# An attention's weights and first products moved ahead of a mixture of experts, and its pair count into another room

## The chip, the cores and the metric

One core of one Trainium2 chip. A time is the device time of one execution in microseconds (us). Engines: PE is TensorE, DVE is VectorE, ACT is ScalarE, POOL is GpSimd, SP is SyncE, which only starts transfers here. Each engine works through its own list of instructions in order, and waits for others by semaphores.

## What is computed

The input `x` is 2 x 1024 x 256. Its rows are normalized (`xn`), and three terms are added.

```python
xn = layernorm(x)
out = x + attention(xn) + ffn(xn)
# attention: tokens of 16 channels; the first 8 attend in windows of 1 x 8 tokens,
# the others in windows of 8 x 1; softmax of q.k / sqrt(8) over the 8 keys of a window,
# plus a depthwise 3x3 convolution of v; then a projection, a norm over the 16 channels, and tok + norm
# ffn: 16 experts of 176 units, of which a row uses 6
scores = sigmoid(xn @ gate.T)
choice = scores + bias                        # the two best of 4 groups, then the 6 best experts of those
w = 2.5 * scores[chosen] / sum(scores[chosen])
y = sum_e w[e] * (silu(xn @ gate_proj[e].T) * (xn @ up_proj[e].T)) @ down_proj[e].T
y += (silu(xn @ shared_gate.T) * (xn @ shared_up.T)) @ shared_down.T
```

## The kernel before

Everything runs in float32 on PE. The program is one straight list in which a scheduler may move an instruction past others on its engine, followed by a short loop at the end for what a list can't hold.

**Load stage.** The 2048 rows lie in 16 tiles of 128. `statistics` and `normalized` (L223, L234) make `xn` and its transpose `xnT`, `logits` (L251) the gate's logits. The attention's small weights come by POOL's transfers (L187 to L203). The shared expert is a generator, `shared_steps` (L263): products `pg` and `pu` on PE, a silu by ACT, `room` (L282) by DVE, and `py` (L288), which ACT writes to a tile `ysh` (L289); four transfers on POOL's queue add it to the output in HBM (L291). `meanwhile(until)` lets it run on beside other work.

**Routing** (L340 to L540) chooses the experts of each row, mostly on DVE in the tile `tmp`, and sorts the rows so that a tile of 128 rows shares six experts as far as possible. Rows with their weights go to HBM (`xw_d`).

**Experts.** `sorted_tile(t)` (L815) gathers one sorted tile by an indirect transfer on POOL's queue (L817, three buffers `xg`), PE turns it (`px_`, L821), ACT copies it, and DVE sorts its weights (L824 to L835). A *slot* is one expert on one tile: `up` (L849) makes `pr_u` on PE (L853, three PSUM buffers), ACT a silu `sg` (L855), DVE the weighted product `hms` (L856). Two slots are a unit; then `hidden` turns `hms` (`ph`, L867), ACT copies it, and the down product `pr_y` follows (L879) one unit later. There are 48 units of sorted tiles, and seven of extra pairs (a row and an expert outside of its tile's six) between tiles 7 and 13. `extras_listed` (L546) counts those pairs in parts of `tmp`; `lists_begun` (L900) then lists them in parts of a tile `ysum`, in steps of its own: ACT copies a column `spot` (L953) out of `at_`, POOL makes two comparison rows (L955, L956), PE adds up `rows_of` (L946). `ysh` and `ysum` have one tag, so they take turns in the same memory; so do `tmp` and the attention's `qk` (tag `qk`).

**Attention.** `weights_prepared` (L576) makes its weights: `qprep` from a product `pqp`, `wq`, `wp`, `rd`, then `mm` and `pb` from two products `pm`, `pbc` from a turned `pb8` (`ppb`), and `lp`. `attention(b, h)` (L653) does one quarter: ACT gathers `rows`, PE makes eight `pq` (L671), each copied by ACT in four pieces (L673 to L676), and DVE does the rest in rows of 2048 elements: `pr` (L684) and `s` (L688) four times, the highest and the exponential (L694 to L696), `pv` (L705) and `o` (L710) four times with the totals between, and `xo` (L718). PE turns `xo` (`po`, L725), ACT copies it to `oT` (L727). After the four quarters `attended` (L761) multiplies by `lp` and `wp` (`pp`, L777), and normalizes.

**The order of the two.** The experts are the main loop; a walk through the attention's steps is laid between the slots. Each step and each slot has a written cost on DVE and on PE; a step is put in when what DVE has been given is no more than `pace` times what PE has been given:

```python
    walk = all_steps()                       # L1084: the weights' eight steps first, then the quarters
    sorted_tile(0)
    meanwhile(100)                           # the rest of the shared expert
    sorted_tile(1)
...
            while step and done[0] <= pace * done[1]:
                step[2]()
                counted(step)
```

`pace` is made from the sums of these costs, so that DVE's and PE's shares end together, up to END = 72 us of PE's, which are left for the last.

## Time and profile before

| what | us |
|---|---|
| three runs | 448.25, 449.36, 454.71 |
| median | 449.36 |
| the profiled execution: its own time | 447.97 |
| its span, first to last instruction | 446.3 |
| PE busy | 393.4 |
| DVE busy | 291.5 |
| ACT busy | 214.1 |
| POOL busy | 197.9 |

A line of the profile gives a start, a length (both us), the engine, the source line, the operation, what it writes and reads with sizes, how often in a row, and in brackets how long the engine had been idle before it and what ended that wait. Busy rows by slices show each fortieth of the span, a digit for tenths. Lengths of rows that follow each other overlap by some 0.07 us, so costs below are taken from start to start where rows are dense. TensorE's granted clock was 0.987 in the mean.

### The profile page before, as it was taken

How to read it: one execution, taken by the hardware profiler on the slowest of the kernel's cores; microseconds unless marked ns; L12 is line 12 of the kernel's file. 1: busy time of each engine (PE TensorE's matmuls, PEld its weight loads, DVE VectorE, ACT ScalarE, POOL GpSimd, SP SyncE). 2: the span in 40 equal slices, each digit the busy share in tenths (PEclk: the TensorE clock that was granted, in tenths of full speed). 3: DMA queues.
4: the chain of work that ended last, by engine and by line, in shares of the span. 5: the costliest groups of instructions: out<-in, count | busy, mean ns of one | idle time of the engine just before them, and what ended most of it. 6: DMA issues, size and time to landing. Idle time of an engine off the chain costs nothing.

```text
span 446.3 us, 6293 instructions
## 1 busy us (share of the span) xinstructions
PE 393.4 (88%) x1668; PEld 246.3 (55%) x1669; DVE 291.5 (65%) x515; ACT 214.1 (48%) x535; POOL 197.9 (44%) x207
## 2 busy tenths in 40 slices
PE   0999999997899788998897999999998899979990
PEld 0435465664466555565564666656665555446670
DVE  4624958635699979289995999959999223322210
ACT  2945258322544442643635456364533657774320
POOL 7300000314273299457524245615554274779432
PEclk9999999999999999999999999999999999998997
DMA  8999941324023101101212124210332101822922
GB/s 232 338 304 321 275 154 30 64 67 86 25 71 73 32 25 34 29 23 33 38 39 60 35 43 81 47 36 24 69 90 56 22 14 57 103 68 74 126 44 24
DMA packets 40178, 37.56 MB, mean 84 GB/s; under 512 B 5300, under 2 KB 37616, under 8 KB 40112
## 3 DMA queue, kind: packets, MB, share of 16 engines
q0 software_dynamic: 11616, 13.52, 18.4%
q1 hardware_dynamic: 27472, 22.59, 16.4%
q10 hardware_dynamic: 1056, 1.05, 0.7%
q8 instruction: 15, 0.25, 0.2%
q14 instruction: 19, 0.16, 0.1%
HBM read 27.70 MB, written 12.45 MB: 90 GB/s over the span
## 4 chain that ended last, share of the span: by engine, by line
DVE 38%; PE 30%; DMA 10%; issue 8%; ACT 7%; POOL 5%; DVEq 0%; POOLq 0%; ACTq 0%; SPq 0%
DVE s L688 6%; PE pr_u L853 6%; DVE pv L705 6%; DVE pr L684 5%; DVE o L710 5%; DVE hms L856 5%; PE pp L777 4%; PE pq L671 3%; PE pr_y L879 3%; DMA out_dram<-ysum,lists 3%; PE pg L273 3%; PE py L288 2%; DMA xg<-xw_d,lists 2%; PE pu L273 2%; DMA xx<-in_x_dram 2%
## 5 line engine op out<-in xcount | busy, mean ns | idle before, releaser
L853 PE MATMUL pr_u<-w1s,xsT 128*128 x384 | 128.4, 468 | 3.4 <-DVE hms L856 2.4
L853 PEld LDWEIGHTS pr_u<-w1s,xsT 128*128 128x128 f32 x384 | 69.9, 191 | 39.4 <-issue 7.7
L994 POOL DMA_INDIRECT out_dram<-ysum,lists x30 | 57.2, 1908 | 77.4 <-ACT ysum L1040 20.3
L855 ACT ACTIVATE sg<-pr_u 128x176 f32<-128x176 f32 x110 | 34.7, 317 | 77.1 <-PE pr_u L853 70.2
L856 DVE SCALAR_TENSOR_TENSOR hms<-sg,w,pr_u 128x176 f32<-128x176 f32 x96 | 36.8, 387 | 35.5 <-ACT sg L855 35.5
L684 DVE TENSOR_TENSOR pr<-qk 128x2048 f32<-128x2048 f32 x16 | 36.6, 2288 | 17.6 <-ACT qk L673 17.2
L705 DVE TENSOR_TENSOR pv<-s,v 128x2048 f32<-128x2048 f32 x16 | 36.5, 2284 | 2.5 <-ACT s L696 2.4
L867 PE MATMUL ph<-ident,hms 128*128 128x128 f32 x165 | 31.7, 282 | 5.5 <-DVE hms L856 2.9
L688 DVE TENSOR_REDUCE s<-pr 128x256 f32<-128x2048 f32 x16 | 36.5, 2279 | 0.1
L955 POOL TENSOR_SCALAR ysum<-row_h,spot 128x128 f16<-128x128 f16 x26 | 28.0, 1094 | 19.2 <-PE rows_of L946 14.9
L710 DVE TENSOR_REDUCE o<-pv 128x256 f32<-128x2048 f32 x16 | 36.3, 2269 | 0.0
L980 POOL DMA_INDIRECT xg<-xw_d,lists x14 | 21.6, 1540 | 29.3 <-DVE hms L856 15.5
L867 PEld LDWEIGHTS ph<-ident,hms 128*128 128x128 f32 x165 | 21.5, 144 | 23.2 <-DVE hms L856 6.9
L291 POOL DMA_DIRECT2D out_dram<-ysh x4 | 3.7, 928 | 64.5 <-ACT ysh L289 64.5
L817 POOL DMA_INDIRECT xg<-xw_d,lists x16 | 19.8, 1239 | 25.4 <-PE ph L867 9.3
L879 PE MATMUL pr_y<-w2a,hT 128*128 x96 | 29.1, 386 | 0.0
L879 PE MATMUL pr_y<-wts,hT 128*128 128x256 f32 x96 | 29.0, 384 | 0.0
L879 PE MATMUL pr_y<-w2b,hT 112*128 x96 | 28.8, 381 | 0.0
L671 PE MATMUL pq<-wq,rows 128*128 128x384 f32 x64 | 25.1, 506 | 3.3 <-ACT oT L727 1.9
L869 ACT COPY hT<-ph 128x384 f32<-128x384 f32 x55 | 26.4, 480 | 2.8 <-PE ph L867 1.8
L853 PE MATMUL pr_u<-w1s,xd 128*128 x56 | 20.4, 487 | 6.6 <-ACT xd L989 6.6
L288 PE MATMUL py<-room 128*128 128x256 f32 x96 | 23.9, 387 | 0.7 <-DVE room L282 0.7
(403 smaller groups left out, 712.2 us busy)
## 6 DMA issues: line engine op xcount, KB each, us to landing
w1s<-in_w_dram SPq DMA_DIRECT2D x22, 256.0 KB, 4.4
wts<-in_w_dram SPq DMA_DIRECT2D x55, 64.0 KB, 2.1
wts<-in_w_dram SPq DMA_DIRECT2D x55, 48.0 KB, 1.7
xw_d<-xx SPq DMA_DIRECT2D x4, 544.0 KB, 4.6
w2a<-in_w_dram SPq DMA_DIRECT2D x4, 512.0 KB, 9.4
out_dram<-ysh POOLq DMA_DIRECT2D x4, 512.0 KB, 5.6
xr<-xw_d POOLq DMA_DIRECT2D x4, 512.0 KB, 5.0
out_dram<-att POOLq DMA_DIRECT2D x8, 256.0 KB, 6.4
```

What stands on the lines that cost most here:

```text
L288: nc.tensor.matmul(py, lhsT=hms[k, m][:, P * c : P * c + P], rhs=w2h[:, m], start=(m == 0), stop=(m == 2))
L671: nc.tensor.matmul(pq.rearrange("p s t c -> p (s t c)"), lhsT=rows[:, i], rhs=wq.rearrange("p s t c -> p (s t c)"), start=True, stop=True)
L684: nc.vector.tensor_tensor(pr, q_.unsqueeze(3).to_broadcast(full), k_.unsqueeze(2).to_broadcast(full), ALU.mult)
L688: nc.vector.tensor_reduce(out=s[:, n : n + NW], in_=held.pop(n), axis=AX.X, op=ALU.add)
L705: nc.vector.tensor_tensor(pr, s[:, n : n + NW].unsqueeze(3).to_broadcast(full), v[:, br, m : m + NW].unsqueeze(2).to_broadcast(full), ALU. ...
L710: nc.vector.tensor_reduce(out=o[:, n : n + NW], in_=held.pop(n), axis=AX.X, op=ALU.add)
L853: nc.tensor.matmul(pu, lhsT=lhs[:, h, :], rhs=w1s[:, :, h, bass.ds(e * I, I)], start=(h == 0), stop=(h == 1))
L855: nc.scalar.activation(sg, pu[:, 0, :], AF.Silu)
L856: nc.vector.scalar_tensor_tensor(hm[:, 0:I], sg, w, pu[:, 1, :], op0=ALU.mult, op1=ALU.mult)
L867: nc.tensor.transpose(ph[:, s, :], units[:, P * s : P * s + P], ident)
L879: nc.tensor.matmul(py, lhsT=l_, rhs=r_, start=start and n == 0, stop=stop and n == 2)
L994: nc.gpsimd.indirect_dma_start(out=out_rows, out_offset=bass.IndirectOffsetOnAxis(ap=index, axis=0), in_=ys, in_offset=None, bounds_check= ...
```

## The change

1. `weights_prepared` is unchanged in itself, but is called whole, right after the load stage and ahead of the first routing row; it was the first eight steps of the walk, beside the first experts.
2. `sorted_tile(1)` and the walk's first steps are put ahead of the rest of the shared expert (`meanwhile(100)`). `done` begins at -LEAD = -12, so the first steps come at once: `gather`, all eight `project`, then `pr`, `s`, `pr`, `s`, `pr`. LEAD is taken out of `pace`, which falls from (273.0 - 18) / (287.8 - 72) = 1.18 to (265.0 - 12 - 18) / (287.0 - 72) = 1.09.
3. `extras_listed` works in parts 4, 5, 6 and 10 of `ysum`, no longer in `tmp` and in a `work` tile; `kept` moves from part 15 to part 7.
4. `ysum` is one tile from the start, used by the shared expert too, where two tiles took turns. So later users wait for the transfers out of their own part only.
5. `at_` is laid out with its three values side by side.

In the list as built, the first six slots come after all eight `pq` of the first quarter (before, `pq` came at slots 5 and 6). Counted by `hms` rows, a quarter's DVE rows reach from 0 to 19, 21 to 40, 44 to 62 and 66 to 84, where they reached from 5 to 26, 29 to 48, 49 to 68 and 69 to 87. `po` is turned at slots 21, 44, 66 and 88, where it was 29, 49, 69 and 88. From slot 88 on the order is the same. On POOL's queue the count's iota and the first write to `at_` now stand behind the third gather, and the shared expert's fourth transfer behind the fifth gather, as before.

```diff
-        ysh = big.tile([P, 16, W], F32, name="ysh", tag="ysum")
+    ysum = big.tile([P, 16, W], F32, name="ysum")
...
+    for _ in weights_prepared():
+        pass
     table_of(AF.Sigmoid, xnT[:, 0, 15, P - 1 : P])
     logits(3)
...
-        upto, mine, more = (tmp[:, n] for n in (2, 5, 7))
+        upto, mine, more = (ysum[:, n].rearrange("p (e t) -> p e t", e=E) for n in (4, 5, 6))
...
-        pair_i = work.tile([P, E * NTL], I32, tag="xd", name="pair_i", bufs=2)
+        pair_i = ysum[:, 10].bitcast(I32)
...
-    kept = ysum[:, 15, 0 : P].bitcast(BF16).rearrange("p (e t) -> p e t", e=E)
+    kept = ysum[:, 7, 0 : P].bitcast(BF16).rearrange("p (e t) -> p e t", e=E)
...
-    at_ = room_[:, 0 : 3 * 257].rearrange("p (a n) -> p a n", a=3)
+    at_ = room_[:, 0 : 3 * 257].rearrange("p (n a) -> p a n", a=3)
...
-    def all_steps():
-        for _ in weights_prepared():
-            yield 1.0, 0.1, lambda: None
-        yield from attention_steps()
...
-    in_walk = [8 * 1.0 + 4 * (16 * 2.3 + 3.3 + 2.5 + 1.5 + 1.4) + 0.6 + 8 * 1.4, 8 * 0.1 + 4 * 6.2 + 8 * 3.9]
-    done = [0.0, 0.0]
+    in_walk = [4 * (16 * 2.3 + 3.3 + 2.5 + 1.5 + 1.4) + 0.6 + 8 * 1.4, 4 * 6.2 + 8 * 3.9]
+    LEAD = 12
+    done = [float(-LEAD), 0.0]
...
-    pace = (whole[0] - END * of_slot["six"][0] / of_slot["six"][1]) / (whole[1] - END)
+    pace = (whole[0] - LEAD - END * of_slot["six"][0] / of_slot["six"][1]) / (whole[1] - END)
...
+    def walked():
+        step = held_.pop()
+        while step and done[0] <= pace * done[1]:
+            step[2]()
+            counted(step)
+            last, step = step, next(walk, None)
+            if last[1] > 1:
+                break
+        held_.append(step)
+
+    walk = attention_steps()
+    held_ = [next(walk)]
     sorted_tile(0)
+    sorted_tile(1)
+    walked()
     meanwhile(100)
-    sorted_tile(1)
```

More of the change, by code (lines that the diff above doesn't have):

```diff
@@ L288, in down @@
                 nc.tensor.matmul(py, lhsT=hms[k, m][:, P * c : P * c + P], rhs=w2h[:, m], start=(m == 0), stop=(m == 2))
-            nc.scalar.activation(ysh[:, 4 * k + c, :], py, AF.Identity, bias=lb)
+            nc.scalar.activation(ysum[:, 4 * k + c, :], py, AF.Identity, bias=lb)
             if c == 3:
-                nc.gpsimd.dma_start(out=by_hl(out_rows)[:, 4 * k : 4 * k + 4, :], in_=ysh[:, 4 * k : 4 * k + 4, :],
+                nc.gpsimd.dma_start(out=by_hl(out_rows)[:, 4 * k : 4 * k + 4, :], in_=ysum[:, 4 * k : 4 * k + 4, :],
                                     accum_op=ALU.add)
@@ L319, in meanwhile, with weights_prepared, centred, banded @@
             spent[1] = next(share)
+    wq = const.tile([P, 3, 8, C], F32, name="wq")
+    wp = const.tile([P, 8, C], F32, name="wp")
+    lp = const.tile([P, 3, 8, C], F32, name="lp")
+    pbc = const.tile([P, 1], F32, name="pbc")
+    def weights_prepared():
+        qp8 = work.tile([4 * C, 8, C], F32, tag="xd", name="qp8", bufs=2)
+        nc.vector.tensor_copy(qp8, qpT.unsqueeze(1).to_broadcast([4 * C, 8, C]))
+        yield
+        pqp = ps_m.tile([P, 4 * C], F32, tag="m", name="pqp")
+        nc.tensor.transpose(pqp, qp8.rearrange("k t c -> k (t c)"), ident[0 : 4 * C, 0 : 4 * C])
+        qprep = const.tile([P, 4 * C], F32, name="qprep")
+        nc.vector.tensor_copy(qprep, pqp)
+        yield
+        qrep, prep = qprep[:, 0 : 3 * C], qprep[:, 3 * C : 4 * C]
+        for s in range(3):
+            nc.vector.tensor_tensor(wq[:, s], qrep[:, C * s : C * s + C].unsqueeze(1).to_broadcast([P, 8, C]),
+                                    band[:, 0, :].unsqueeze(2).to_broadcast([P, 8, C]), ALU.mult)
+        yield
+        def centred(v):
+            m = small.tile([P, 1], F32, tag="cm", name="cm")
+            nc.vector.tensor_reduce(out=m, in_=v, axis=AX.X, op=ALU.add)
+            nc.vector.tensor_scalar(m, m, 1.0 / C, None, op0=ALU.mult)
+            nc.vector.tensor_scalar(v, v, m, None, op0=ALU.subtract)
+        centred(prep)
+        centred(pb)
+        yield
+        nc.vector.tensor_tensor(wp, prep.unsqueeze(1).to_broadcast([P, 8, C]),
+                                band[:, 0, :].unsqueeze(2).to_broadcast([P, 8, C]), ALU.mult)
+        rd = const.tile([C, 5, C], F32, name="rd")
+        nc.vector.tensor_tensor(rd, prep[0:C, :].unsqueeze(1).to_broadcast([C, 5, C]),
+                                tp.unsqueeze(2).to_broadcast([C, 5, C]), ALU.mult)
+        wvr = work.tile([C, 2, 8, C], F32, tag="xd", name="wvr", bufs=2)
+        nc.vector.tensor_copy(wvr[:, 0], wvT.unsqueeze(1).to_broadcast([C, 8, C]))
+        nc.vector.tensor_copy(wvr[:, 1].rearrange("p t c -> p (t c)"), cbc.to_broadcast([C, P]))
+        yield
+        pm = ps_m.tile([P, 6, C], F32, tag="m", name="pm")
+        nc.tensor.matmul(pm[:, 0:5, :].rearrange("p d c -> p (d c)"), lhsT=wvr[:, 0].rearrange("p t c -> p (t c)"),
+                         rhs=rd.rearrange("p d c -> p (d c)"), start=True, stop=True)
+        nc.tensor.matmul(pm[:, 5, :], lhsT=wvr[:, 1].rearrange("p t c -> p (t c)"), rhs=prep[0:C, :], start=True,
+                         stop=True)
+        nc.vector.tensor_tensor(pb, pb, pm[:, 5, :], ALU.add)
+        mm = const.tile([P, 5, C], F32, name="mm")
+        nc.vector.tensor_copy(mm, pm[:, 0:5, :])
+        yield
+        ppb = ps_m.tile([P, P], F32, tag="m", name="ppb")
+        pb8 = work.tile([P, 8, C], F32, tag="xd", name="pb8", bufs=2)
+        nc.vector.tensor_copy(pb8, pb.unsqueeze(1).to_broadcast([P, 8, C]))
+        nc.tensor.transpose(ppb, pb8.rearrange("p t c -> p (t c)"), ident)
+        nc.vector.tensor_copy(pbc, ppb[:, 0:1])
+        yield
+        part = work.tile([P, 2, 8, C], F32, tag="xd", name="part", bufs=2)
+        def banded(to, tap, d):
+            nc.vector.tensor_tensor(to, mm[:, tap, :].unsqueeze(1).to_broadcast([P, 8, C]),
+                                    band[:, d, :].unsqueeze(2).to_broadcast([P, 8, C]), ALU.mult)
+        banded(lp[:, 0], 1, 0)
+        banded(part[:, 0], 0, 1)
+        banded(part[:, 1], 2, 2)
+        banded(lp[:, 1], 3, 0)
+        banded(lp[:, 2], 4, 0)
+        nc.vector.tensor_tensor(lp[:, 0], lp[:, 0], part[:, 0], ALU.add)
+        nc.vector.tensor_tensor(lp[:, 0], lp[:, 0], part[:, 1], ALU.add)
+        yield
@@ L573, in extras_listed @@
         yield
-    def weights_prepared():
-        qp8 = work.tile([4 * C, 8, C], F32, tag="xd", name="qp8", bufs=2)
-        nc.vector.tensor_copy(qp8, qpT.unsqueeze(1).to_broadcast([4 * C, 8, C]))
-        yield
-        pqp = ps_m.tile([P, 4 * C], F32, tag="m", name="pqp")
-        nc.tensor.transpose(pqp, qp8.rearrange("k t c -> k (t c)"), ident[0 : 4 * C, 0 : 4 * C])
-        qprep = const.tile([P, 4 * C], F32, name="qprep")
-        nc.vector.tensor_copy(qprep, pqp)
-        yield
-        qrep, prep = qprep[:, 0 : 3 * C], qprep[:, 3 * C : 4 * C]
-        for s in range(3):
-            nc.vector.tensor_tensor(wq[:, s], qrep[:, C * s : C * s + C].unsqueeze(1).to_broadcast([P, 8, C]),
-                                    band[:, 0, :].unsqueeze(2).to_broadcast([P, 8, C]), ALU.mult)
-        yield
-        def centred(v):
-            m = small.tile([P, 1], F32, tag="cm", name="cm")
-            nc.vector.tensor_reduce(out=m, in_=v, axis=AX.X, op=ALU.add)
-            nc.vector.tensor_scalar(m, m, 1.0 / C, None, op0=ALU.mult)
-            nc.vector.tensor_scalar(v, v, m, None, op0=ALU.subtract)
-        centred(prep)
-        centred(pb)
-        yield
-        nc.vector.tensor_tensor(wp, prep.unsqueeze(1).to_broadcast([P, 8, C]),
-                                band[:, 0, :].unsqueeze(2).to_broadcast([P, 8, C]), ALU.mult)
-        rd = const.tile([C, 5, C], F32, name="rd")
-        nc.vector.tensor_tensor(rd, prep[0:C, :].unsqueeze(1).to_broadcast([C, 5, C]),
-                                tp.unsqueeze(2).to_broadcast([C, 5, C]), ALU.mult)
-        wvr = work.tile([C, 2, 8, C], F32, tag="xd", name="wvr", bufs=2)
-        nc.vector.tensor_copy(wvr[:, 0], wvT.unsqueeze(1).to_broadcast([C, 8, C]))
-        nc.vector.tensor_copy(wvr[:, 1].rearrange("p t c -> p (t c)"), cbc.to_broadcast([C, P]))
-        yield
-        pm = ps_m.tile([P, 6, C], F32, tag="m", name="pm")
-        nc.tensor.matmul(pm[:, 0:5, :].rearrange("p d c -> p (d c)"), lhsT=wvr[:, 0].rearrange("p t c -> p (t c)"),
-                         rhs=rd.rearrange("p d c -> p (d c)"), start=True, stop=True)
-        nc.tensor.matmul(pm[:, 5, :], lhsT=wvr[:, 1].rearrange("p t c -> p (t c)"), rhs=prep[0:C, :], start=True,
-                         stop=True)
-        nc.vector.tensor_tensor(pb, pb, pm[:, 5, :], ALU.add)
-        mm = const.tile([P, 5, C], F32, name="mm")
-        nc.vector.tensor_copy(mm, pm[:, 0:5, :])
-        yield
-        ppb = ps_m.tile([P, P], F32, tag="m", name="ppb")
-        pb8 = work.tile([P, 8, C], F32, tag="xd", name="pb8", bufs=2)
-        nc.vector.tensor_copy(pb8, pb.unsqueeze(1).to_broadcast([P, 8, C]))
-        nc.tensor.transpose(ppb, pb8.rearrange("p t c -> p (t c)"), ident)
-        nc.vector.tensor_copy(pbc, ppb[:, 0:1])
-        yield
-        part = work.tile([P, 2, 8, C], F32, tag="xd", name="part", bufs=2)
-        def banded(to, tap, d):
-            nc.vector.tensor_tensor(to, mm[:, tap, :].unsqueeze(1).to_broadcast([P, 8, C]),
-                                    band[:, d, :].unsqueeze(2).to_broadcast([P, 8, C]), ALU.mult)
-        banded(lp[:, 0], 1, 0)
-        banded(part[:, 0], 0, 1)
-        banded(part[:, 1], 2, 2)
-        banded(lp[:, 1], 3, 0)
-        banded(lp[:, 2], 4, 0)
-        nc.vector.tensor_tensor(lp[:, 0], lp[:, 0], part[:, 0], ALU.add)
-        nc.vector.tensor_tensor(lp[:, 0], lp[:, 0], part[:, 1], ALU.add)
-        yield
@@ L645, in csw_block_moe @@
-    wq = const.tile([P, 3, 8, C], F32, name="wq")
-    wp = const.tile([P, 8, C], F32, name="wp")
-    lp = const.tile([P, 3, 8, C], F32, name="lp")
-    pbc = const.tile([P, 1], F32, name="pbc")
     oT = big.tile([P, 4, 2, 4, P], F32, name="oT", tag="oT")
@@ L803, in csw_block_moe @@
     xsT = big.tile([P, NTL, 2, P], F32, name="xsT", tag="xx")
-    ysum = big.tile([P, 16, W], F32, name="ysum", tag="ysum")
     xflat = ysum.rearrange("p n d -> p (n d)")[0:1, 8 * W : 8 * W + 3 * NXM].bitcast(I32)
     xrow = xflat.rearrange("p (a n) -> p a n", a=3)
-    kept = ysum[:, 15, 0 : P].bitcast(BF16).rearrange("p (e t) -> p e t", e=E)
+    kept = ysum[:, 7, 0 : P].bitcast(BF16).rearrange("p (e t) -> p e t", e=E)
     wsrt = route.tile([P, NTL, E], F32, name="wsrt")
@@ L1082, in counted @@
             done[n] += cost[n]
-    walk = all_steps()
+    def walked():
[9 more added lines that the diff above has]
+    held_ = [next(walk)]
     sorted_tile(0)
+    sorted_tile(1)
+    walked()
     meanwhile(100)
-    sorted_tile(1)
     tiles_sorted = 2
-    step = next(walk)
     laid_out = list(units())
@@ L1119, in csw_block_moe @@
             counted(of_slot[laid_out[min(u, len(laid_out) - 1)][0]])
-            while step and done[0] <= pace * done[1]:
-                step[2]()
-                counted(step)
-                last, step = step, next(walk, None)
-                if last[1] > 1:
-                    break
+            walked()
             if done_:
```

## Prediction

> **What bounds the kernel now.** I read the busy row by slices first, then VectorE's (DVE's) busy time stage by stage, then DVE in order of time.

> ```profile
> span 446.3 us, 6293 instructions
> PE   0999999997899788998897999999998899979990
> DVE  4624958635699979289995999959999223322210
> ```

> PE looks full nearly everywhere and DVE only from slice 10 on (one slice is 11.2 us). But PE's rows are pipelined and a digit hides short waits, so the middle has to be asked for by stage. I cut it at the attention's four quarters: from the first product row `pr` (L684) of a quarter to the end of its last row `xo` (L718), and the gap to the next `pr`. The columns are stretch, its length, DVE busy (instructions), granted PE clock, DMA share, GB/s.

> ```profile
> 98.00:119.05 21.05, 10.62 (x50) 0.92 0.27 59
> 119.05:179.07 60.02, 56.25 (x88) 1.00 0.19 45
> 179.07:188.05 8.98, 1.11 (x5) 1.00 0.18 28
> 188.05:238.54 50.49, 48.13 (x47) 1.00 0.17 36
> 238.54:244.27 5.73, 0.31 (x1) 1.00 0.25 59
> 244.27:292.09 47.82, 46.83 (x41) 1.00 0.27 52
> 292.09:297.96 5.87, 0.40 (x2) 1.00 0.23 34
> 297.96:345.63 47.67, 46.65 (x41) 1.00 0.26 56
> ```

> Inside a quarter DVE is 94 to 98% busy: it sets the pace. Between quarters it is idle for 5.7 to 9.0 us, while PE turns `xo` (L725), ACT copies, and PE makes the next `pq` (L671). Before the first quarter, from 98 to 119, it is half idle. So up to the last `po` at 345.68 the time is 98 + 21 + four quarters + three gaps; the last 100.6 us (after 345.68) belong to PE, ACT, POOL and the final adds, with DVE at 2 tenths.

> Why does DVE start only at 119? DVE and PE in order of time:

> ```profile
> 102.15 0.23 DVE L588 COPY qprep<-pqp 128x64 f32<-128x64 f32 x1 [5.85 <-PE pqp L586]
> 107.62 0.42 DVE L551 SCALAR_TENSOR_TENSOR ysum<-tmp,extras 128x256 bf16<-128x256 f32 x1 [2.52 <-DMA xg<-xw_d,lists]
> 110.23 0.45 PE L627 MATMUL ppb<-ident,pb 128*128 128x128 f32 x1 [2.76 <-DVE pb L626]
> 119.05 2.29 DVE L684 TENSOR_TENSOR pr<-qk 128x2048 f32<-128x2048 f32 x1 [1.72 <-ACT qk L673]
> ```

> The weights' chain waits behind the experts' start (5.85), L551 waits at 107.6, just as the last shared sum's out DMA (issued 101.95, 5.54 to land) frees the tile that `kept` lies in, PE waits for `pb8` (2.76), and `tmp`, whose room `qk` needs, is read until 116.

> **The change, part by part.**

> *Weights into the load stage.* They issue no DMA; their inputs are on the chip by 21.8 (DVE's wait at L612 ends there). DVE: from `qprep` to `rd` 102.15 to 104.95 with 0.5 of other work inside, so 2.3; then `pb`, `mm`, `pb8` 0.4 and `lp` 1.5: 4.2 us into DVE's idle 7.74 between 31.6 and 39.3. PE: `pqp` 0.27, `pm` twice 0.3, `ppb` 0.45, about 1.2 us, into a PE that is full there (5.00 busy of 33 to 38). In the new order the `room` row L284 stands behind the `lp` rows and ahead of L424, the first routing row, and waits for a `pu` that PE now ends 1.2 later (40.4 for 39.2). Routing thus starts 1.0 to 1.2 later, and its DVE chain from 40 to 57 is dense: **+1.2** as far as the first gathered tile. Without the idle cover it would be 4.2 more. From 101 to 110 the same PE work goes, with the 2.76 wait.

> *Pairs counted in ysum.* `tmp` is free once routing ends, so `qk` is. The scan now waits only for the second out DMA, long landed; the iota waits for the third (issued 83.98 before, 5.6 to land): about 91, with two gathers behind it on POOL, which wait for buffers until 92.5 anyway. Cost 0, up to 1. The strided writes of `at_` by ACT (0.41 each) and DVE have no row: between 0 and one doubling of three rows, 1.2; I take 0, the nearest rows being of equal size.

> *First products ahead of the experts.* PE: the first tile's transposes at 90.91+1.2 = 92.1, two tiles 0.8, half `pg` 0.86, two `pq` 1.3, half `pg` 0.9, two `pq` 1.3: 97.2; ACT's copies of the fourth `pq` (four at 0.16) end at 97.9. First `pr` at **98.0, 21.05 earlier**. Price: the last shared `room` row on DVE now stands behind `pr` and `s` (4.5 us), to 103.1; PE reaches `py` at 101.4 and stalls about 0.8; 20 records at 0.22 end it at 107.5. The first expert starts 6.9 later than 100.56. Queued behind: the fourth out DMA on POOL, and behind that the gather of tile 5 (about 111, landing 114; PE wants it at about 114.4). But 5.3 us of `pq`, 1.2 of weights and the waits of 2.76 and 1.27 are gone from what follows, so slot 6 (each `pr_u` of a routed expert is a slot) starts at about 120, against 124.63.

> *First quarter.* DVE's 60.0 before, plus the `room` row 0.6, plus sorting rows of four more tiles (two groups of three rows at 0.3, four copies at 0.1: 2.2), less two `hms` rows of 0.31: **62.2, +2.2**, with its 3.3 of waits kept.

> *Pace.* It falls from 1.18 to 1.09 DVE us per PE us. The order of instructions shows where this goes: a quarter's rows stand as close to the `hms` rows as before (18 or 19 slots), and the room lies in the gaps. `xo` to `po` is 3, 1, 1 and 1 slots before, and 2, 4, 4 and 4 after. In a gap PE bounds: after the last `hms` it must do `ph` 0.64, `pr_y` 1.3, two `pr_u` 2.6, `ph` and `pr_y` 1.9 ahead of `po`, 6.4, of which 1.2 lie under `xo`: 5.2 more than a gap of before with one slot. Gaps: first, with two slots for three, 7.5 for 8.98 (**-1.5**); second 10.9 for 5.73 (**+5.2**); third, with part of an extra pair (4.9 for 4.2) in it, 11.3 for 5.87 (**+5.4**); `xo` to the last `po` 5.2 for 0 (**+5.2**). The bounds are 0 (PE has run ahead) and 6.4 each. The slots done there at PE's own pace are why this is only half a loss: it is already in the sum, since the number of slots ahead of the last `po` is 88 in both.

> [...] The gathers are issued by POOL:

> ```profile
> 128.63 0.95 POOL L817 DMA_INDIRECT xg<-xw_d,lists  x1 [0.30 <-PE ph L867]
> 130.53 3.08 POOL L817 DMA_INDIRECT xg<-xw_d,lists  x1 [0.95 <-DVE wsrt L824]
> 135.61 0.95 POOL L817 DMA_INDIRECT xg<-xw_d,lists  x1 [0.74 <-PE px__1336 L821]
> ```

> 0.95 alone, 3.08 beside a `pr` row (130.51 to 132.80), 0.95 beside an `s` row (134.60 to 136.87). [...] After the change eleven gathers lie beside `pr` and `pv` rows. [...] By the trace it is hidden: three buffers mean that PE wants a tile 3.6 slots, some 9 us, after it frees the buffer, and 3.1 of issue plus 3.0 of landing are 6.1. I take 0; with the cover gone it is the slower rival.

> *Sum:* -21.05 + 2.2 - 1.5 + 5.2 + 5.4 + 5.2 = -4.5 (the +1.2 is in the 98.0). The tail has the same order in both. The profiled execution took 447.97 (1.7 around its span), so 443.4; the median shown is 449.36, 1.4 above it. I keep to the profiled execution, which two of the three runs shown lie within 1.4 of: **443.5**.

> **The rivals.**

> *The gaps close up.* If PE runs further ahead of DVE, the gaps stay at 5.8 and the last `po` follows `xo` at once: 15.8 less, 428; half of it is likelier, 436. For it: PE's plain pair of slots takes 4.2 (217.33 to 221.55) where DVE's takes 5.0 (201.20 to 206.21). Against: three `pr_u` buffers hold PE within three slots of DVE.

> *The late first expert is not made up.* If slots keep their mean pace, 245.1 from the first `pr_u` to the last `po` less 8 for the moved `pq` with its waits, the last `po` comes at 107.5 + 237 = 344.6: 447. For it: PE shows 45.3 of 47.8 busy in the third quarter. Against: the 5.0 per pair is DVE's.

> *Slower: the gathers.* If issue and landing pass the time from freeing a buffer to its use (about 9 us), each of the eleven gathers holds PE, and DVE with it: at 1.6 of the 2.1 each, 443 + 18 = 461. [...]

> **How the numbers follow.** The likeliest 0.50 (its own range 437 to 450), closing gaps 0.18, not made up 0.20, slower 0.12. From 434 to 453 leaves out the far half of the first rival (0.08) and most of the slower one (0.11). Two per cent, about what a measurement tells here, is 440.4 and 458.3. Below lie most of the first rival (0.16) and some of the likeliest (0.14), 0.30; above, the gathers, 0.11; between 0.59.

> **What would show it.** Right: the first `pr` near 98, the first `pr_u` near 107.5, no L551 or `ppb` wait, the last `po` near 341, DVE gaps of 7 to 11 us between quarters, a tail of 100 us. Wrong: `px` waits on gathers between 110 and 140, quarters much over 48 us, or routing more than 2 us late at the first gather.

## The result, and the profile after

| | us |
|---|---|
| before, median of 20 runs | 449.31 (447.73 to 454.71) |
| after, median of 20 runs | 454.41 (453.43 to 456.27) |
| after over before | 1.011, 95% interval 1.0091 to 1.0128 |
| predicted | 443.5 (434 to 453) |
| span profiled, before and after | 446.3 and 453.0 |
| first `pr`, before and after | 119.05 and 99.07 |
| last `xo` ends | 345.63 and 346.41 |

The kernel after is 5.1 us slower. The attention did start 20 us sooner, and its last row on VectorE (DVE) still ends 0.8 us later than before. First the busy rows by slices of the kernel after:

```profile
PE   0999999998896978989799979899999899979990
DVE  4627958689896945899838989469997223331210
```

DVE's digits are high from slice 8 on, where before they were from 10 on, and the holes behind the quarters are longer. DVE's busy time in the stretches of the kernel after, cut as in the prediction (quarter, gap, and so on, from the first `pr`; then from the last `xo` to the last `po`, and the tail). The columns are stretch, length, DVE busy (instructions), granted clock of TensorE (PE), DMA share, GB/s:

```profile
99.07:163.49 64.42, 58.39 (x95) 0.95 0.22 49
163.49:175.04 11.55, 1.08 (x6) 0.85 0.04 10
175.04:227.10 52.06, 47.14 (x42) 1.00 0.15 31
227.10:238.91 11.81, 3.01 (x9) 1.00 0.25 56
238.91:286.60 47.69, 46.43 (x41) 1.00 0.27 51
286.60:298.73 12.13, 1.42 (x5) 1.00 0.28 55
298.73:346.41 47.68, 46.42 (x41) 1.00 0.25 54
346.41:351.23 4.82, 1.82 (x7) 1.00 0.38 53
351.23:453.00 101.77, 23.09 (x48) 0.95 0.37 59
```

The third and fourth quarters are the length that they were (47.69 and 47.68; 47.82 and 47.67 before). The 20 us were lost in the first two quarters (4.40 and 1.57 longer) and in the three gaps (14.9 longer in sum); the step to the last `po` costs another 4.8, and the tail 1.2. The clock is below 1 in the first quarter, the first gap and the tail. PE in order of time shows waits that are at most 0.6 us each in the kernel before; the brackets hold the idle time and what ended it:

```profile
104.33 4.15 PE L290 MATMUL py<-room 128*128 128x256 f32 x18 [1.71 <-DVE room L284]
116.14 0.41 PE L823 MATMUL px__1148<-ident,xg 128*128 128x128 f32 x2 [1.65 <-DMA xg<-xw_d,lists]
141.26 0.50 PE L823 MATMUL px__1384<-ident,xg 128*128 128x128 f32 x2 [3.83 <-DMA xg<-xw_d,lists]
164.52 0.17 PE L948 MATMUL rows_of<-ysum 128*128 128x26 f16 x1 [3.14 <-POOL ysum L958]
```

A shared sum, two gathered tiles and the list of extra pairs each come after PE wants them. With 0.66 at 124.90 the gathers cost 6.1 us of PE's time.

One more view is needed: the time by slots. A slot is an `hms` row on DVE, one for each expert on a tile; there are 110, and the n-th is the same piece of expert work in every kernel. I read the starts of these rows from DVE in order of time. A column compares like with like only where the same steps of the attention lie ahead of that slot; from slot 88 on they do, but for the run with the old pace.

| start of slot | 1 | 6 | 20 | 24 | 44 | 88 | 110 |
|---|---|---|---|---|---|---|---|
| before, us | 102.4 | 121.3 | 163.8 | 174.7 | 227.9 | 345.9 | 431.7 |
| after, less before | +8.7 | +0.7 | +0.2 | +11.9 | +4.2 | +4.2 | +5.2 |

At slot 20 the two are level, and the attention of the kernel after is ahead: its first quarter ended at 163.49, that of before at 179.07. By slot 44 four us are lost, and from there nothing changes. Between slots 20 and 88 DVE has 146.9 us to do in the kernel after and 158.3 in that of before, 11 less; PE is busy for 169.7 of 186.2 us and for 166.7 of 182.2. With less to do on DVE, the stretch takes 4.0 longer. PE's work didn't shrink. Of the 6.7 us between the two spans, 5.2 are there at slot 110; the other 1.5 come behind it.

### The profile page after: what moved, and what is told of

It reads as the page before. It is cut to its first block, busy times and chain, and to the rows that moved or that the text cites. A ratio compares the mean times of both kernels' runs of the same rounds, so it can differ in the third digit from the quotient of the medians.

```text
span 453.0 us, 6294 instructions
## 1 busy us (share of the span) xinstructions
PE 396.2 (87%) x1668; PEld 248.4 (55%) x1669; DVE 292.2 (65%) x515; ACT 215.2 (48%) x535; POOL 189.1 (42%) x207
## 4 chain that ended last, share of the span: by engine, by line
PE 40%; DVE 24%; DMA 12%; issue 8%; POOL 7%; ACT 6%; POOLq 0%; SPq 0%; DVEq 0%; ACTq 0%
PE pr_u L855 9%; PE pr_y L881 5%; DVE pv L709 5%; DVE pr L688 4%; DVE s L692 4%; PE pg L275 4%; DMA out_dram<-ysum,lists 4%; PE pp L781 4%; PE py L290 4%; DVE o L714 4%; PE pu L275 4%; DMA out_dram<-att 4%; DVE hms L858 3%; PE pq L675 3%; DMA xg<-xw_d,lists 3%
## 5 line engine op out<-in xcount | busy, mean ns | idle before, releaser
L855 PE MATMUL pr_u<-w1s,xsT 128*128 x384 | 132.0, 476 | 2.4 <-DVE hms L858 1.9
L996 POOL DMA_INDIRECT out_dram<-ysum,lists x30 | 51.3, 1711 | 88.3 <-ACT ysum L1035 36.1
L688 DVE TENSOR_TENSOR pr<-qk 128x2048 f32<-128x2048 f32 x16 | 36.6, 2287 | 15.6 <-ACT qk L677 10.9
L293 POOL DMA_DIRECT2D out_dram<-ysum x4 | 3.7, 921 | 78.7 <-ACT ysum L291 78.7
L869 PE MATMUL ph<-ident,hms 128*128 128x128 f32 x165 | 30.3, 281 | 6.1 <-ACT hT L871 3.6
L869 PEld LDWEIGHTS ph<-ident,hms 128*128 128x128 f32 x165 | 21.8, 145 | 24.1 <-issue 8.0
L982 POOL DMA_INDIRECT xg<-xw_d,lists x14 | 20.1, 1437 | 23.9 <-DVE hms L858 15.5
L855 PE MATMUL pr_u<-w1s,xd 128*128 x56 | 21.4, 507 | 7.3 <-ACT xd L991 7.3
L819 POOL DMA_INDIRECT xg<-xw_d,lists x16 | 19.3, 1204 | 18.6 <-PE pr_u L855 6.7
```

The source lines that it names most:

```text
L688: nc.vector.tensor_tensor(pr, q_.unsqueeze(3).to_broadcast(full), k_.unsqueeze(2).to_broadcast(full), ALU.mult)
L855: nc.tensor.matmul(pu, lhsT=lhs[:, h, :], rhs=w1s[:, :, h, bass.ds(e * I, I)], start=(h == 0), stop=(h == 1))
L869: nc.tensor.transpose(ph[:, s, :], units[:, P * s : P * s + P], ident)
L996: nc.gpsimd.indirect_dma_start(out=out_rows, out_offset=bass.IndirectOffsetOnAxis(ap=index, axis=0), in_=ys, in_offset=None, bounds_check= ...
```

## The experiments

Theory A: the prediction's sum is right in kind, DVE's stretches add up to the time, and single waits brought by the head start made the loss. Theory B: PE's slots set the end, and a head start for DVE turns into idle time of DVE. Each ratio is to the kernel before on the same chip, with its 95% interval.

### Parts of the change, and three changes of one thing

`e_room`: parts 3 to 5 alone, no other edit.

> The kernel before with the third, fourth and fifth part of the change alone: pairs are counted in ysum, ysum is one tile, at_ is laid out anew; the weights stay in the walk and the walk starts with the experts. Theory A (the loss comes from single waits that the head start brought: the spot copies that hold ACT in the first gap, gathers, more slots in the gaps): the room part is free or a gain; the wait of L551 (2.5 us) and the wait for tmp ahead of the first pr go, 445 to 449. Theory B (PE's own work sets the end of the quarters, and what DVE gains early becomes idle time of DVE): the first pr comes some 3 us earlier, and the last po stays within 1 us of 345.7, 448.5 to 450. If the room part itself costs (the strided writes of at_, ACT held by POOL): over 451.

Measured 452.60, ratio 1.0092 (1.0058 to 1.0125): the room alone costs as much as the whole change. DVE and then PE of this kernel in order of time:

```profile
97.61 0.36 DVE L832 TENSOR_TENSOR wf<-e6b,row_f 128x192 f32<-128x192 f32 x1
97.89 0.68 DVE L284 TENSOR_TENSOR room<-room,pu 128x512 f32<-128x512 f32 x1
```

```profile
98.62 1.56 PE L290 MATMUL py<-room 128*128 128x256 f32 x6 [2.22 <-DVE room L284]
```

Freed from their wait, the counting rows (L554 to L565 of this kernel) run early, ahead of the last shared `room` row. It starts at 97.89, where it started at 95.62, PE waits 2.22 for it, and slot 1 is 2.2 late. Slot 6 is 4.2 late, two steps at half clock (below) lying between, and it stays at 3.8 to 4.2 to the last slot. It is the third case of the expectation, for a reason that the expectation doesn't name.

`e_nowalk`: the kernel after without the early products (with LEAD at 0, `pace` is 1.15).

```diff
-    LEAD = 12
+    LEAD = 0
...
     sorted_tile(0)
-    sorted_tile(1)
-    walked()
     meanwhile(100)
+    sorted_tile(1)
```

> The kernel after with LEAD = 0 and the first steps of the walk behind the shared expert again, as before: weights early and the new room are kept, the early products are not. Theory A: against before, +1.2 in the routing, and about 5 less where the weights' chain stood beside the first experts (the waits of 2.76 and 2.5): 445 to 448, and most of the loss of the kernel after is gone. Theory B: PE has the same work, 1.2 of it earlier; the last po comes within 2 us of 346: 448 to 451. If the loss is of the weights in the load stage: 453 or more.

Measured 459.64, 1.0236 (1.0174 to 1.0299). The early products are not what costs: without them the rest of the change is worse. Its first quarter takes 69.3 us, with waits of 3.29 for a gather and 3.03 for `rows_of`.

`e_spot26`: `spot` gets `bufs=NX` (26) in `pair_listed`.

> The kernel after with a buffer for each of the 26 spot columns, so that ACT copies them all without a wait for POOL. Theory A: in the first gap ACT's sg and oT no longer stand behind eight copies that wait 0.83 us each; the gap falls from 11.55 to about 7.5, and the time by 4: 450 to 451. Theory B: PE is 9.15 of 11.55 busy there, so at most 2.4 can go, and what goes comes back as idle time of DVE in the second gap: 453 to 455.

Measured 456.36, 1.0183 (1.0142 to 1.0224). The copies bunch up on ACT and `oT` comes behind 23 of them: the first gap is 17.6 us for 11.55, the second quarter 47.8 for 52.06, and slot 44 stands at +4.3, as in after. Theory A's cause for the first gap, the copies' waits for a buffer, falls in this form. ACT's order in that gap in the kernel after:

```profile
169.62 0.19 ACT L955 COPY spot<-ysum 128x3 f32 x1 [0.83 <-POOL ysum L958]
169.72 0.31 ACT L857 ACTIVATE sg<-pr_u 128x176 f32<-128x176 f32 x1
```

The `sg` behind the last of eight such copies is what DVE waited 5.37 us for; removing the copies' waits moved the delay, it didn't remove it.

`e_pace`: the old pace with the head start.

```diff
-    pace = (whole[0] - LEAD - END * ...
+    pace = (whole[0] + 8.0 - END * ...
```

> The kernel after with the pace of before (about 1.19 for 1.09), head start kept: the walk's steps come earlier against the slots, po at slots 20, 39, 58 and 78 for 21, 44, 66 and 88, so the last ten slots of the quarters move behind them. Theory A with DVE as the bound inside a quarter: four gaps of one or two slots, quarters of 48, the last po about 15 us earlier, at 336, and the ten slots come in the tail, where PE alone works, at 3.2 each if the tail has no room for them (454 to 458), for nothing where it has (440). Theory B: the quarters stay at 48 to 52 with shorter gaps, the last po comes near 325, ten slots of 2.1 to 2.6 us on PE follow in the tail, and the sum is within 2 us of after: 452 to 456.

Measured 453.65, 1.0121 (1.0089 to 1.0154). DVE's busy time in its quarters and gaps:

```profile
98.09:160.25 62.16, 57.48 (x92) 0.95 0.22 51
160.25:169.76 9.51, 1.70 (x10) 0.85 0.04 12
169.76:219.56 49.80, 46.94 (x41) 0.99 0.14 30
219.56:225.44 5.88, 1.86 (x5) 1.00 0.00 0
225.44:273.80 48.36, 46.84 (x42) 1.00 0.26 50
273.80:279.60 5.80, 0.40 (x1) 1.00 0.32 68
279.60:327.24 47.64, 46.63 (x41) 1.00 0.26 55
```

Here the head start arrives: quarters and gaps are within 2.2 us of those of before, and the last `xo` ends at 327.24, 18.4 sooner. But `po` is turned ten slots earlier, at slot 78 for 88, and the ten slots between follow behind it: from the last `po` to the end of the span it is 122 us, where before it is 100, 2.2 more for each of the ten slots. Slot 110 starts at 432.2, 0.5 later than before; 3.3 more come behind it. So theory B holds here; the attention was early, and the slots were not.

### Which engine sets the pace

`e_before_dve_less` sums half of the channels in `s` (half of each q.k is left out); `e_before_pe_less` leaves out the middle term of every pair's down product. Both start from the kernel before.

```diff
-            ... in_=held.pop(n), axis=AX.X, op=ALU.add)
+            ... in_=held.pop(n)[:, :, :, :, 0 : HD // 2], axis=AX.X, op=ALU.add)
```

> The kernel before, with the s rows summing only half of the products' channels (half of each q.k is left out): DVE does 16 rows of about 1.15 us in place of 2.28, some 18 us less, 4.5 in each quarter. If DVE sets the pace inside a quarter, as the prediction has it: quarters of 43 to 44 us for 47.8, the last po 18 earlier, 431. Theory G (PE sets the end): the last po within 2 us of 345.7, DVE idle for what it saves, 447 to 450.

> The kernel before, with the middle one of the three terms of every pair's down product left out (48 products of 0.43 us on PE, 20.8 us in all, 37 of them ahead of the last po). If DVE sets the pace inside a quarter: the last po stays near 345, and only the 11 products of the tail go, 4.7 us: 443 to 445. Theory G: the last po comes 14 to 16 earlier, and the whole is 428 to 431, if no new windows at half clock come with DVE's waits.

With 17 us less on DVE (274.4 busy for 291.5): 451.25, 1.0042 (1.0018 to 1.0067). DVE's stretches in that kernel:

```profile
117.71:177.76 60.05, 51.31 (x84) 0.94 0.19 43
177.76:189.50 11.74, 2.11 (x8) 1.00 0.16 31
189.50:236.71 47.21, 43.58 (x45) 0.96 0.16 34
236.71:244.78 8.07, 1.02 (x5) 1.00 0.34 69
244.78:289.60 44.82, 42.29 (x39) 0.96 0.23 43
289.60:301.34 11.74, 1.50 (x5) 1.00 0.37 66
301.34:344.26 42.92, 41.86 (x39) 1.00 0.24 55
```

The quarters got 11.0 us shorter and the gaps 11.0 longer (31.55 for 20.58), and PE is busy for 11.05 and 11.04 of the two long gaps. What DVE saves inside a quarter, it waits in the gap behind it. With 20.8 us less on PE: 459.42, 1.0247 (1.0199 to 1.0296), no gain either. Its quarters take 62.7, 51.2, 48.6 and 47.2 us, so they did not get shorter in sum: inside a quarter DVE does set the pace. PE is idle for 71.5 us in place of 52.9, and half clock (below) takes 14.6 for 3.3; how much of the slower time is due to which is not separated. The two engines are balanced in this order: relief of one alone brought nothing. Both of my expectations for the second, 428 to 431 and 443 to 445, were wrong.

### Half clock after a wait

PE's granted clock falls to 0.50 in single stretches. PE's busy time in the kernel before, in steps of 3.41 us:

```profile
103.13:106.54 3.41, 3.00 (x14) 1.00 0.99 164
106.54:109.96 3.42, 0.93 (x4) 1.00 0.22 81
109.96:113.37 3.41, 3.14 (x11) 0.50 0.03 5
113.37:116.78 3.41, 2.52 (x8) 1.00 0.30 82
```

The step with the wait for `ppb` is busy for 0.93 us, and the next runs at half clock throughout. In the records of the clock such a step lasts 3.413 us, and in the kernel before two of them begin at 109.955 and 403.502, 86 such lengths apart. In all 20 kernels profiled here they start on one grid of 3.413 us in each execution. I fitted the grid to them and counted 2264 steps at full clock up to 430 us, where the clock is on record:

| PE busy in a step of 3.41 us | steps | next step at half clock |
|---|---|---|
| up to 1.45 us | 65 | 65 |
| 1.46 to 1.75 | 35 | 10 |
| 1.76 to 2.00 | 41 | 1 |
| over 2.00 | 2123 | 0 |

Theory G: these steps make the loss. With them PE's span splits into its work (busy time less half of that at half clock, for in the kernel after products of 128 x 128 start 0.21 us apart there and 0.11 at full clock), that half, and idle time: before 390.2 + 3.3 + 52.9, after 389.5 + 6.8 + 56.7. Work is equal within 0.7; in these two executions 3.5 us come from half clock and 3.8 from waits. The same split in one stretch, from 85 us, just ahead of the first gather, to slot 44:

| 85 us to slot 44, us | length | PE's work | half clock | idle |
|---|---|---|---|---|
| before | 142.9 | 126.4 | 1.6 | 14.9 |
| after | 147.1 | 123.2 | 5.1 | 18.7 |
| `e_tiles3_sf` (below) | 144.0 | 122.9 | 2.8 | 18.3 |
| `e_t3sf_first8` (below) | 137.2 | 122.0 | 0.0 | 15.1 |

This stretch decides: from slot 44 to slot 110 each of the 20 kernels but `e_pace` takes 202.5 to 205.6 us. The kernel after has 3.2 us less work on PE there, and loses those and 4.2 more to waits and half clock. I then filled waits with products of no use.

`e_warm` (besides, 14 ahead of the first `rows_of`), and the same line ahead of `ppb` (`e_before_warm`) and of one `pr_u` in the tail (`e_before_tail`):

```diff
         px_ = ps_m.tile([P, 2, P], F32, tag="m", name="px_")
+        for _ in range({5: 8, 14: 16}.get(t, 0)):
+            nc.tensor.matmul(px_[:, 0, :], lhsT=ident, rhs=ident, start=True, stop=True)
...
```

> The kernel after with filling products on PE in front of three of its long waits, each into a tile that the next real product overwrites: 8 of 128 x 128 ahead of the turn of the sixth sorted tile (PE waited 1.65 us there), 16 ahead of that of the fifteenth (3.83), 14 ahead of the first rows_of (3.14). The order of everything else is the same. Theory G (new): PE's own work sets the end, and each long wait of PE is followed by one window of 3.42 us at half clock, which costs 1.71 more; the kernel after has three such windows ahead of 400 us, the kernel before one. G expects the windows at 117, 141 and 165 us gone, the waits still there, and 3.5 to 5 us less than after: 449.5 to 451. Theory A (single waits alone, DVE or ACT late): filling can only cost, 454 to 457.

> The kernel before with 12 filling products of 128 x 128 in front of the turn of pb8 (ppb), where PE waited 2.76 us; all else as before. Theory G: the one window at half clock between 109 and 114 us goes, and 1.7 us with it: 446 to 447 where before takes 448 to 449. If windows don't come from waits, or PE's time doesn't set the end: 448 to 450.

> The kernel before with 8 filling products of 128 x 128 on PE (1.7 us) ahead of the gate and up product of the thirteenth extra pair in the tail, where PE waited 2.21 us for ACT at 400.2 to 402.4; nothing else is moved. Theory G: the window at half clock at 403.5 goes in nearly every execution, 1.5 us less: 447 to 447.8 where before takes 449. If the half clock comes from elsewhere, or isn't on the path: no change, or up to 1.7 more where the wait is shorter than the filling.

`e_warm`: 455.36, 1.0143 (1.0104 to 1.0181), after 1.011. The three steps at half clock that it aimed at are gone, but a wait of 3.58 for another gather is followed by one at 124, and one of 2.09 for `hT` by one at 216. (The list put the first `rows_of` a slot earlier too, so the order wasn't quite the same.) `e_before_warm`: 452.18, 1.0065 (1.0041 to 1.0089), slower; `rows_of` now waits 4.01. `e_before_tail`: 448.94, 1.0001 (0.9978 to 1.0024); the step at 403.5 is gone, and the time is the same. Nor does the clock tell the kernels apart over many executions: the median is 0.978 for before (80 executions) and 0.976 for after (20), some 1 us of PE's time. The profiled execution of before, at 0.987, was one of its best. So half clock is a cost that rides on the waits; by itself it isn't the cause.

### Where the waits come from

Theory L: the late last shared sum heads the chain. Theory B3: the gathers are held by their three buffers. `e_shared_first` swaps `walked()` and `meanwhile(100)`; `e_tiles3_sf` also turns the third tile early; `e_tiles3` does that without the swap; `e_tiles3_sf_warm` adds 12 fillings ahead of the fifteenth tile and of `rows_of`.

```diff
-    sorted_tile(0)
-    sorted_tile(1)
+    AHEAD = 2
+    for t in range(AHEAD + 1):
+        sorted_tile(t)
+    meanwhile(100)
     walked()
-    meanwhile(100)
...
-                sorted_tile(tiles_sorted)
+                if tiles_sorted > AHEAD:
+                    sorted_tile(tiles_sorted)
```

> The kernel after with one change of order: the rest of the shared expert is put ahead of the attention's first steps, so that the last room row no longer stands behind pr and s on DVE, nor py behind it on PE. The first pr comes some 2 us later. Theory L (the late shared sum heads the chain: py waits 1.71, the fourth out DMA goes at 109.3 where it went at 101.95, the gathers behind it are late): the waits of py and of the gathers go, and with them two of the three windows at half clock: 449 to 451. Theory B3 (the gathers are held by their three buffers: the sixth tile's gather waits for the third tile's turn, at 109.5, whatever stands ahead of it on POOL): the waits for gathers stay near 6 us, one or no window goes, 452 to 455.

> As the run with the shared expert first, and besides the third sorted tile is gathered and turned ahead of the first expert, so that its buffer is free some 13 us earlier and the sixth tile's gather goes at about 97. Theory B3: the gather waits at 116 and 125 go (2.3 us), that of the fifteenth tile stays; at most two windows ahead of 400: 449 to 451.5. Theory L: no more than with the shared expert first alone.

> As the run before it in this set, with 12 filling products of 128 x 128 on PE ahead of the turn of the fifteenth tile and 12 ahead of the first rows_of, 2.6 us each. Theory G (a window of 3.41 us in which PE is busy for less than half is followed by one at half clock): the windows near 141 and 165 us go, up to 3.4 us less than without the filling, less what the filling delays: 447 to 450. If PE doesn't wait at these two places any more, each filling costs its 2.6: 453 to 455.

> The kernel after, with the third sorted tile gathered and turned ahead of the attention's first steps, the shared expert behind them as in after. Theory B3 (gathers held by their three buffers): the waits of 1.65 and 0.66 us at 116 and 125 go, and the window at 117; 450.5 to 452.5. If the fourth out DMA ahead of them on POOL holds the gathers: 453.5 to 455.5.

Measured 461.50 (1.0239, 1.0183 to 1.0295), 452.26 (1.0095, 1.0059 to 1.0130), 459.85 (1.0250, 1.0211 to 1.0290) and 456.79 (1.0162, 1.0128 to 1.0195). Theory L falls: the shared expert first is 7 worse than after. PE now waits 2.77 for `room` with no `pq` to fill it, and half clock takes 11.1 us for 6.8. Turning the third tile early is worth 9.2 beside the swap: the waits for gathers fall from 7.6 to 5.2, and half clock from 11.1 to 4.5. Without the swap it costs 2.4, with a wait of 3.21 for `room` and 4.21 for a gather. So theory B3 holds in one order and not in the other. The fillings of the third run cost 7.6 more (11.3 in the profiled executions), outside of both cases of its expectation: 6.0 of work, and half clock at 11.3 for 4.5, with two steps at 99 us, ahead of any filling.

POOL's price shows in one gather of the kernel after. POOL and DVE at the fifteenth tile, for which PE waits 3.83 at 141.26:

```profile
136.10 3.13 POOL L819 DMA_INDIRECT xg<-xw_d,lists  x1 [2.50 <-PE pr_u L855]
136.12 2.27 DVE L709 TENSOR_TENSOR pv<-s,v 128x2048 f32<-128x2048 f32 x1
```

The gather could start only at 136.10, when its buffer came free, and then took 3.13 in place of 0.95. In the 20 kernels 30 of 320 gathers of sorted tiles took over 1.9 us; each of them lies beside a `pr` or `pv` row, and lasts 0.8 to 1.1 us beyond the time that it shares with that row. The mean of all sixteen (1204 ns in after, 1239 before) hides this: before, PE did not wait for the tile whose gather took 3.08.

`e_weights`: part 1 alone (`pace` is 1.15 in it, too). `e_weights_t3`: with the second and third tiles ahead of the shared expert.

> The kernel before with the first part of the change alone: the attention's weights are made in the load stage, the room of the pair count and the order of the walk stay. By the prediction's terms: +1.2 in the routing, -1.2 and -2.76 where PE waited for ppb beside the first experts: 446 to 447. Theory G: PE reaches the gathered tiles sooner than their gathers allow (the weights' work and the first pq lay between them), so that the wait of ppb comes back as waits for gathers, with a window at half clock: 449 to 453.

> The weights alone, and the second and third sorted tiles gathered and turned ahead of the rest of the shared expert. Theory B3: the waits for gathers that the weights alone bring are shorter by the time that the buffers are free earlier, 2 to 4 us, and with them one window at half clock: 446 to 449, the best of these. If gathers don't matter: within 1 us of the weights alone.

Measured 467.39 (1.0409, 1.0371 to 1.0447) and 465.24 (1.0341, 1.0302 to 1.0380). DVE of `e_weights`:

```profile
108.20 0.43 DVE L630 SCALAR_TENSOR_TENSOR ysum<-tmp,extras 128x256 bf16<-128x256 f32 x1 [3.78 <-DMA out_dram<-ysh]
```

With the weights' rows gone from DVE, this row (L551 of before) comes sooner and waits 3.78 for the shared sum's transfer in place of 2.52; the `hms` rows behind it hold PE for 2.60, `pq` waits 2.59 and the gathers 5.2. The first quarter takes 73.9 us; in the whole, PE's idle time is 9.2 more than before, and half clock 9.5 more. The two tiles turned early gain 2 us. So the parts don't add: the weights alone cost 18 us, with the new room 12, and with the early products besides 5.

`e_first8`, its control `e_before_first8` on the kernel before, and `e_t3sf_first8` (with the third tile early and the swap) list the pairs later, outside of the first gap:

```diff
-FIRST = 7
+FIRST = 8
...
-            if i in (2, 4, 8) or i >= 14:
-                next(extras_ if i < 14 else lists_, None)
+            if i in (2, 4, 8) or i >= 20:
+                next(extras_ if i < 20 else lists_, None)
```

> The kernel after with the listing of the extra pairs begun at slot 20 in place of 14, and the extra pairs one tile later (behind tiles 8 to 14); nothing else. The spot copies then lie one in a slot behind the first gap between quarters, and no rows_of stands ahead of it. If the listing in the gap is what costs: PE's wait of 3.14 us ahead of rows_of, the window at half clock near 165 and ACT's late oT go, slot 44 is level with before: 449.5 to 451. If PE's own work sets the stretch from slot 20 to 88 whatever DVE has to do, but the listing doesn't matter: 453.5 to 455.5, the wait found elsewhere.

> Control: the kernel before with the same later listing. There PE waited 0.58 us ahead of rows_of and 2.42 for an hms behind listing rows of DVE at 150 us. If the listing costs only where it falls into a gap: 448 to 450, as before. If moving it gains by itself: 446 to 447.5.

> The later listing together with the shared expert first and the third tile turned early (which took 452.3). If the two causes are separate, the gains add: 448 to 450, level with before or a little better; if PE's waits only move: 452 to 454.

Measured 464.66 (1.0353, 1.0300 to 1.0406), 464.32 (1.0348, 1.0301 to 1.0395) and 453.68 (1.0140, 1.0079 to 1.0202). The edit has a cost of its own, which I had not seen. POOL of `e_first8` at the end:

```profile
442.41 1.53 POOL L996 DMA_INDIRECT out_dram<-ysum,lists  x1 [2.89 <-ACTq L1142]
446.88 1.54 POOL L996 DMA_INDIRECT out_dram<-ysum,lists  x1 [2.94 <-DMA out_dram<-ysum,lists]
451.33 1.54 POOL L996 DMA_INDIRECT out_dram<-ysum,lists  x1 [2.91 <-DMA out_dram<-ysum,lists]
454.76 1.54 POOL L996 DMA_INDIRECT out_dram<-ysum,lists  x1 [1.89 <-DMA out_dram<-ysum,lists]
```

Transfers out follow each other at 3.4 to 4.5 us, the last three each waiting for the one before, and with extra pairs one tile later they are still in line when PE is done: from slot 110 to the end all three take 24.8 to 25.4 us, before 14.6. So I compare slot 110: `e_first8` 436.9, after 436.9; the control 438.5, before 431.7; `e_t3sf_first8` 425.9, `e_tiles3_sf` 433.5. The same edit gains nothing, costs 6.8 or gains 7.6, by the order that it is put into.

In `e_first8` the listing's cost moved. The first gap is 11.5 us as in after, but PE is busy for 10.77 of it (9.15 in after, in part at half clock), and the quarter ahead of it takes 59.70 for 64.42. Then ACT's copies of `pq` stand behind three `spot` copies that wait for POOL (2.24, 0.61 and 0.83), PE waits 4.07 for them, and the second quarter takes 59.19 for 52.06:

```profile
171.60 0.19 ACT L955 COPY spot<-ysum 128x3 f32 x1 [2.24 <-POOL ysum L958]
```

`e_t3sf_first8` differs from `e_tiles3_sf` by the later listing alone. First quarter, first gap and second quarter on DVE, of `e_tiles3_sf` and then of `e_t3sf_first8`:

```profile
106.98:165.01 58.03, 56.66 (x91) 1.00 0.23 53
165.01:177.70 12.69, 1.05 (x6) 0.73 0.11 17
177.70:227.17 49.47, 46.79 (x42) 1.00 0.14 31
106.43:160.44 54.01, 52.63 (x73) 1.00 0.23 55
160.44:168.38 7.94, 5.40 (x23) 1.00 0.03 8
168.38:218.56 50.18, 46.73 (x41) 1.00 0.17 33
```

Here PE's wait of 3.05 for `rows_of` and two steps at half clock are gone from the gap, and it falls to 7.94: in this order the listing in the gap was what cost. The kernel has no step at half clock ahead of slot 88 but one, its idle time up to slot 44 is that of before (table above), and slot 110 stands 5.8 ahead of the kernel before. There the head start pays; its time does not show it, for the 10 us at the end. The profiled execution is one of the three shortest of its six (452.0 to 452.4; the others took 454.9 to 457.9).

## Why the prediction was wrong

- *What held.* The sum took back most of the early start by itself: with the second and third gap and the step to the last `po`, 15.8 us, which came true within 0.9 each. The 4.5 that it kept is what PE had idled in the stretch saved (98 to 119 in the kernel before, PE busy):

```profile
98.00:119.05 21.05, 16.61 (x63) 0.92 0.27 59
```

- *The step that failed: PE's waits, put at nothing.* The sum has the gathers at 0, the waits of 2.76 and 1.27 as gone (they went, and others came), the first gap at -1.5, and no term for half clock. Up to slot 44 PE had 3.2 us less work and was idle for 18.7 us in place of 14.9, with 5.1 lost to half clock in place of 1.6. So 7.3 us came where 4.0 were to go, more than the 4.5 that the sum kept.
- *"Inside a quarter DVE is 94 to 98% busy: it sets the pace."* Right for the length of a quarter: less work on PE did not shorten them. As the ground for adding up DVE's stretches it failed: 17 us less on DVE made shorter quarters and longer gaps. PE is busy for 53.27, 45.21, 45.34 and 44.38 us of the same quarters of before, which leaves it little room to make up a wait.
- *First `pr` 21.05 earlier.* It came 19.98 earlier (99.07 for 98.0). `e_pace` shows the term alone: 18.4 at the last `xo`, nothing at the last slot.
- *Against the sum's 443.4 the profiled execution took 454.7.* By terms: first `pr` +1.1, first quarter +2.2 (64.42 for 62.2), first gap +4.05 (11.55 for 7.5), second quarter +1.6, second gap +0.9, third +0.8, last `xo` to last `po` -0.4, tail +1.1.
- *Gathers at 0, with three buffers as the cover.* Wrong: 6.1 us of waits, because the `pq` and the weights that lay between the tiles were gone, so PE came to the sixth tile 5.0 us after the third (at 114.49, for 109.50; 9.5 before). The longer gathers beside `pr` and `pv` rows, weighed as the slower rival, have a part in it. Its 2.1 for each is one row of before less another (3.08 less 0.95). Of the eleven gathers from 110 us on ten took 0.95 to 1.80, and one, issued beside a whole `pv` row, 3.13; about 2.2 of the 3.83 that PE waited for its tile are an estimate of that part (3.13 less the 0.95 of a gather alone). Why a gather takes longer there is not shown by any run.
- *First gap -1.5.* Wrong in sign. PE waited 3.14 for `rows_of` and 1.32 for `oT`, and one step ran at half clock. The listing of pairs lies behind all three. Moving it made the gap 4.75 shorter in `e_t3sf_first8`; in `e_first8`, the order of after, the cost came back in the second quarter. That it alone sets this gap in after is not shown.
- *Second and third gap, last `po`:* right within 0.9. *Routing +1.2:* right (first gather at 87.09 for 85.87). *No wait of L551 or `ppb`:* right. *The first expert at 107.5:* 108.32. *Slot 6 at about 120, against 124.63:* the product at 124.63 is the seventh slot's; it came at 122.89, 1.7 sooner for the 4.6 that were forecast. *Strided writes of `at_`:* 0.49 for 0.41 on DVE, nothing. *Pairs counted in `ysum`, cost 0 to 1:* wrong in the room alone, +2.2 by DVE's order, and by slot 20 half clock takes 2.8 more than before.
- *The rival "the late first expert is not made up"*: its cause isn't seen, for slot 6 was only 0.7 late; but its premise, that slots keep their pace on PE, is what held.

What stays open: how much of the 5.1 belongs to which wait. Nearly every edit that took one wait away brought another, so the runs show the sum (idle time +3.8, half clock +3.5 in the profiled executions; over many executions the clock differs by some 1 us only), not its shares. A kernel with the waits of `e_t3sf_first8` and the transfers out as before was not run.

## What to carry to other kernels

Before counting an earlier start as a gain, ask for the busy time of every engine in the stretch that it saves: count what the busiest one idles there (4.4 of 21 us here), not what the waiting one does. Then ask what that engine will wait for once it comes sooner. Where two engines are both nearly full (here DVE for 94 to 98% of a quarter and PE for 89 to 95%), take some work from each in turn on the chip; if neither gives anything, look at the waits between them. An edit that takes work out from between two loads or transfers can uncover them (here 6.1 us of waits for gathers). Count in units of the main loop (slots), not only in stretches of one engine.
